# The end of an attention and mixture-of-experts kernel on one core: the turn of the head ahead of the last, the last output copy, and the place of a loop with a run-time count

## The chip, the cores and the metric

The kernel runs on one core of one Trainium2 chip. A core has a matrix engine (TensorE, PE in the rows), a vector engine (VectorE, DVE), an activation engine (ScalarE, ACT), a general engine (GpSimd, POOL) and an engine that mostly issues transfers (SyncE, SP). All of them run their own instruction streams and meet through semaphores. The metric is the device time of one execution in microseconds; the time before is the median of three runs.

## The reference, cut to what matters

```python
# x: (8, 512, 256); attention with 4 groups of 4 query heads, D = 128; experts: 64, the best 6 of each token, room 64
x = x + _layernorm(_L0_attn_ref(_layernorm(x), wq, bq, wkv, bkv, wo))
x = x + _layernorm(_L0_ffn_ref(_layernorm(x), gate_w, w_gate, w_up, w_down, sh_gate, sh_up, sh_down))

# attention: q = x @ wq + bq + pe ; k, v from x @ wkv + bkv (k + pe)
scores = jnp.einsum('bgqtd,bgksd->bgqts', q, k) / math.sqrt(D)          # causal mask follows
probs = jax.nn.softmax(scores, axis=-1)
out = jnp.einsum('bgqts,bgksd->btgqd', probs, v).reshape(b, t, G * QPG * D) @ wo

# feed-forward: softmax over x @ gate_w.T, best 6 experts of each token; each expert takes its first 64 tokens
g = jax.nn.silu(jnp.einsum('ech,ehf->ecf', buf, w_gate)); u = jnp.einsum('ech,ehf->ecf', buf, w_up)
d = jnp.einsum('ecf,efh->ech', g * u, w_down)                            # weighted and added back to the tokens
y = y + (jax.nn.silu(h @ sh_gate.T) * (h @ sh_up.T)) @ sh_down.T         # the shared expert
```

## The kernel before

There are 8 sequences ("batches" below) of 512 tokens and 16 heads, so 128 pairs of batch and head, which the main loop numbers k = 0 to 127. One pass of that loop computes the scores of head k in four row tiles (`scores`, L328: product, mask and minimum on VectorE, exponential with row sums on ScalarE), turns the weights of head k - 1, weighs head k by the reciprocal row sums (`weigh`, L345; on VectorE for the last head alone), projects head k - 3 into the sums of its batch (`project`, L402), computes the queries of head k + 1 and multiplies the turned weights of head k - 2 with the values (`mix`, L390).

Turning means that the weights, tokens in rows, have to stand with keys in rows. For most heads `turned` does it with block transposes on VectorE and a pass through DRAM: four stores `ex_d<-eb` and one load `et<-ex_d` on SP. For the last two heads, 126 and 127, `turned_at_once` transposes on TensorE (L380): ten 128x128 transposes in four groups of 4, 3, 2 and 1, each group into one PSUM buffer of the pool `ps_s`, which has three. ScalarE copies groups 0 and 2 out, VectorE groups 1 and 3. The fourth group therefore waits for the buffer of the first. In the pass of head 127 this call for head 126 stands behind the scores and ahead of `project(124)`. After the loop come `mix(126)`, the projections of 125 and 126, the turn of 127, its product with the values, the copy of that product to SBUF (`ao`, on ScalarE, 128x512) and its projection.

`last_part` then does the feed-forward of the last batch, number 7, mixed with what is left of batch 6. All instructions there stand in a hand-written order (`manual_schedule`), and each engine runs its own in that order. For batch 7: normalization, the shared expert in three chunks of the hidden size (`shared`, L749 and L762; its product with the down matrix in three parts, L728), the routing, and the one pair of experts with free places ("late"): `gather` and `gate_up`, `hid_late`, `turn_hidden` (`pth_late`, `ht_late`), `down` (`pd_late`, then `dd_late` copied by ScalarE), and the last products that add it to the sums `py` (L952). `output6` is a generator that finishes batch 6 in three steps: statistics (VectorE) and the power -0.5 (GpSimd); shift, four scaled rows (ScalarE, L98) and four additions (GpSimd, L694); and the store (SP, L696). In the kernel before, all three steps are called behind `down("late")`, and the generator's last chunk of the shared expert (`next(f)`, the VectorE operations `gs` and `hid` of chunk 0) ahead of them.

At the very end, if more than one pair of experts has free places, a loop with a run-time count (`tc.For_i(0, table["rest"], 1)`, L1073) goes over these other pairs. Each pass recomputes the outputs of batches 5, 6 and 7, so the kernel keeps for it in DRAM the residuals (`x1_d`), the rows with scores and places (`lxg_d`) and the sums (`ly_d`) of those batches. With the inputs given, the count is zero: no line of its body is in the trace. What remains of it is the way around it, on every engine. In the program, SP waits at the way around for the eight semaphores of the transfers that SP and ScalarE issue, then each engine walks a list of twelve waits (all transfers, all engines and their sequencers), and branches on. Behind it stands only the program's end: SP waits for what is open, each engine drains, and two rounds of a barrier follow (L1148).

Of the kernel before, what the change touches and what calls it, by code (L numbers as in the profile page):

```python
# [16 lines left out]
ALU = mybir.AluOpType  # L17
AX = mybir.AxisListType

P = 128  # L20
B, T, E = 8, 512, 256
NT = B * T
NI = T // P
BS = 32
AT = [0, 4, 7, 9]
# [14 lines left out]
EARLY = 5  # L40
# [4 lines left out]
def sandwich_kernel(ctx, tc, x, wq, bq_t, wkv, bk_t, bv, wo, gate_wt, w_gate, w_up, w_down,  # L45
# [63 lines left out]
    def on_act(dst, src):  # L109
        nc.scalar.copy(dst, src)  # L110
# [35 lines left out]
    with ExitStack() as part:  # L146
# [226 lines left out]
        def turned_at_once(k):  # L373

            l = live[k]
            l["et"] = p2.tile([P, NI, NB, BS], F32, tag="et", name=f"et_{k}")
            for j in range(NI):
                pt = ps_s.tile([P, NI, NI, BS], F32, tag="s", name=f"pe_{k}_{j}")
                for i in range(j, NI):
                    nc.tensor.transpose(pt[:, i - j, :, :].rearrange("p a t -> p (a t)"), l["e"][i][:, ts(j, P)], ident)  # L380
                (on_act, on_dve)[j % 2](l["et"][:, :, AT[j] : AT[j] + NI - j, :].rearrange("p a n t -> p n a t"),
                                        pt[:, : NI - j, :, :])

        def mix(k):
            b, h = divmod(k, NH)
            l, g = live[k], h // QPG

            pav = ps_m.tile([P, NI, NI, BS], F32, tag="m", name=f"pav_{k}")
            for j in range(NI):
                nc.tensor.matmul(pav[:, :, j:, :], lhsT=seqs[b]["v"][:, j, ts(g, D)],  # L390
                                 rhs=l["et"][:, :, AT[j] : AT[j] + NI - j, :], start=j == 0, stop=j == NI - 1)
            l["ao"] = p2.tile([D, T], F32, tag="ao", name=f"ao_{k}")
            on_act(l["ao"].rearrange("d (i a t) -> d i a t", i=NI, a=NI), pav.rearrange("d a i t -> d i a t"))
# [492 lines left out]
        def last_part(before, spare):  # L886
# [34 lines left out]
            nc.sync.dma_start(out=rows_of(x1_d, b * T), in_=xt)  # L921
# [18 lines left out]
            next(f)  # L940
# [3 lines left out]
            gate_up_hidden("late")  # L944
            turn_hidden("late")
            l["part"](py, 0)
            down("late")
            output6()
            output6()
            output6()  # L950
            for i in range(NI):
                nc.tensor.matmul(py[i // 2][:, i % 2, :], lhsT=gt[:, ts(i, P)], rhs=pairs["late"]["dd"],  # L952
                                 start=False, stop=True, skip_group_check=True)
            mv, rs = norm_scales([py[i // 2][:, i % 2, :] for i in range(NI)], f"y{b}")
            y = p2.tile([P, NI, E], F32, tag="xnt", name=f"y_{b}")
            for n in range(2):
                nc.scalar.copy(y[:, ts(n, 2), :], py[n])
            nc.sync.dma_start(out=rows_of(ly_d, b * T - ET_ROWS), in_=y)
            for i in range(NI):
                nc.vector.tensor_scalar(o[:, i, :], py[i // 2][:, i % 2, :], mv[:, i, 0:1], None, ALU.subtract)  # L960
            for i in range(NI):
                nc.vector.scalar_tensor_tensor(xt[:, i, :], o[:, i, :], rs[:, i : i + 1], xt[:, i, :],
                                               ALU.mult, ALU.add)
                if i % 2:
                    nc.sync.dma_start(out=rows_of(out, b * T)[:, i - 1 : i + 1, :], in_=xt[:, i - 1 : i + 1, :])
# [32 lines left out]
        for k in range(NK):  # L998
# [10 lines left out]
            if k == NK - 1:  # L1009
                turned_at_once(k - 1)  # L1010
            weigh(k)
            side(s, "A")
            if k >= 3:
                project(k - 3)
# [53 lines left out]
        last_part(behind, routed)  # L1068
# [4 lines left out]
        with tc.For_i(0, table["rest"], 1) as n:  # L1073
# [5 lines left out]
            for b in range(EARLY, B):  # L1079
# [3 lines left out]
                q, tag = [(p1, "y"), (p2, "x"), (p2, "x")][b - EARLY]  # L1083
# [8 lines left out]
            for b in range(EARLY, B):  # L1092
# [7 lines left out]
                for _ in output(b, y, residual(b, p1, "xn")):  # L1100
                    pass

# [49 lines left out]
```

## Time and profile before

| what | value |
|---|---|
| median of three runs | 1431.27 us (1430.13 to 1436.82) |
| profiled execution, its own time | 1429.28 us |
| its span, first to last instruction | 1427.6 us |
| granted TensorE clock, mean over the span | 0.994 |
| TensorE busy | 1383.4 us, 97% of the span |
| VectorE, ScalarE, GpSimd busy | 63%, 35%, 30% |
| last matmul starts / last store issued / last store landed | 1411.8 / 1416.8 / 1420.9 us |

Rows of the timeline give the start, the duration or length of a merged group, the engine, the line, the operation, output and inputs by the program's names with shapes, and in brackets how long the engine stood idle before and what released it. In the table of stretches the numbers after the stretch are its length and then the busy time of PE, PE's weight loads, VectorE, ScalarE and GpSimd, each with its count of instructions; after them the granted clock, the share of DMA time and GB/s. Rows of one line's instructions give a count, the shortest, median and longest duration in ns, and the first and last start. Times of landing are those of the trace's records of transfers, on the same clock.

### The profile page before, as it was taken

What the parts mean: (1) busy time and instruction counts of PE and PEld (TensorE: products, weight loads), DVE (VectorE), ACT (ScalarE), POOL (GpSimd) and SP (SyncE); (2) the same over time, 40 slices, a digit from 0 to 9 for tenths busy, and PEclk for the clock granted to TensorE, in tenths of its full rate; (3) what the DMA queues carried; (4) which work ended last, traced back from release to release, by engine and by line L of the source; (5) the groups of instructions that cost most, each with busy time, mean ns of one, the idle gap of its engine ahead of it and who ended that gap; (6) DMA issues with size and microseconds to landing.
All of it is one profiled execution on the core that took longest, in us unless ns stands there. A gap on an engine that the chain in (4) does not pass through costs nothing.

```text
span 1427.6 us, 18526 instructions
## 1 busy us (share of the span) xinstructions
PE 1383.4 (97%) x5230; PEld 841.4 (59%) x5230; DVE 895.4 (63%) x3127; ACT 500.2 (35%) x1432; POOL 433.7 (30%) x698
## 2 busy tenths in 40 slices
PE   9999999999999999999999999999989999999895
PEld 5665665666556665656556665655546565556463
DVE  5565577656775577557765677566656545677634
ACT  2332344224332334234422433233433333444421
POOL 2222242213321242114221232124545344444311
PEclk9999999999999999999999999999999999999998
DMA  7774566546763576455654566459999889877702
GB/s 243 204 225 146 140 181 198 146 119 171 215 177 107 150 208 193 110 140 164 207 164 125 155 173 193 107 147 276 302 246 258 225 239 252 210 236 250 240 30 82
DMA packets 167990, 262.50 MB, mean 184 GB/s; under 512 B 17212, under 2 KB 142109, under 8 KB 167885
## 3 DMA queue, kind: packets, MB, share of 16 engines
q1 hardware_dynamic: 133069, 212.00, 50.5%
q10 hardware_dynamic: 28672, 39.85, 9.4%
q0 software_dynamic: 6144, 9.44, 3.4%
q8 instruction: 42, 0.69, 0.2%
q14 instruction: 63, 0.52, 0.1%
HBM read 148.25 MB, written 112.99 MB: 183 GB/s over the span
## 4 chain that ended last, share of the span: by engine, by line
PE 80%; DMA 7%; DVE 7%; issue 2%; ACT 2%; POOL 1%; SPq 1%; ACTq 0%; DVEq 0%; POOLq 0%
PE pav L390 16%; PE psc L328 15%; PE pq L315 13%; PE po L402 13%; PE pk L285 4%; PE pv L296 4%; PE psg L749 3%; PE psu L749 3%; PE pgu L590 2%; PE py L776 2%; PE pd L616 2%; DMA wd<-in_w_down 2%; DVE eb L361 1%; DMA exr_d<-xb_f 1%; ACT e L335 1%
## 5 line engine op out<-in xcount | busy, mean ns | idle before, releaser
L345 POOL TENSOR_SCALAR e<-e,recip 128x128 f32<-128x128 f32 x508 | 268.5, 574 | 757.6 <-DVE recip L342 744.0
L335 ACT ACTIVATE e<-e,least 128x128 f32<-128x128 f32 (+3 forms) x512 | 285.8, 559 | 349.2 <-DVE least L332 337.1
L328 PE MATMUL psc<-kt,qt 128*128 128x128 f32 (+3 forms) x1024 | 306.3, 438 | 8.6 <-DVE least L332 6.0
L390 PE MATMUL pav<-et,v 128*128 128x512 f32 (+3 forms) x1024 | 297.5, 434 | 3.3 <-DMA et<-ex_d 3.0
L390 PEld LDWEIGHTS pav<-et,v 128*128 128x128 f32 x1024 | 194.1, 190 | 165.7 <-issue 116.8
L332 DVE CUSTOM_DVE_ANT_0 e<-psc,mask 128x128 f32<-128x128 f32 (+3 forms) x512 | 232.6, 479 | 56.3 <-PE psc L328 49.4
L402 PE MATMUL po<-wo_sb,ao 128*128 128x256 f32 x1024 | 243.5, 381 | 0.7 <-ACT ao L110 0.7
L315 PE MATMUL pq<-xnt,wq_sb 128*128 128x512 f32 x512 | 242.2, 596 | 0.0
L402 PEld LDWEIGHTS po<-wo_sb,ao 128*128 128x128 f32 x1024 | 193.1, 190 | 72.0 <-issue 41.0
L110 ACT COPY ao<-pav 128x512 f32<-128x512 f32 x128 | 74.9, 585 | 443.8 <-PE pav L390 429.6
L361 DVE STREAM_TRANSPOSE eb<-e 128x128 f32<-128x128 f32 x756 | 227.4, 364 | 3.5 <-DMA ex_d<-eb 3.2
L328 PEld LDWEIGHTS psc<-kt,qt 128*128 128x128 f32 x1024 | 164.6, 191 | 76.7 <-DVE least L332 26.9
L318 DVE SCALAR_TENSOR_TENSOR qt<-pq,bq_sb,pe_sb 128x512 f32<-128x512 f32 x128 | 95.6, 747 | 104.6 <-PE pq L315 104.4
L315 PEld LDWEIGHTS pq<-xnt,wq_sb 128*128 128x128 f32 x512 | 96.3, 191 | 69.7 <-issue 64.3
L342 DVE RECIPROCAL recip<-total 128x4 f32<-128x4 f32 x128 | 22.8, 178 | 120.2 <-ACT e L335 120.2
L335 ACT ACTIVATION_READ_ACCUMULATOR e<-e,least 128x1 f32 x512 | 95.8, 187 | 0.0
L627 POOL DMA_INDIRECT y_d<-dd,idx x32 | 50.9, 1591 | 102.0 <-DMA y_d<-dd,idx 51.5
L285 PE MATMUL pk<-xnt,wkv_sb 128*128 128x512 f32 x128 | 59.3, 594 | 0.2 <-ACT xnt L110 0.2
L296 PE MATMUL pv<-wkv_sb,xnt 128*128 128x512 f32 x128 | 58.1, 593 | 0.0
L298 DVE TENSOR_TENSOR v<-pv,bv_sb 128x512 f32<-128x512 f32 x32 | 22.1, 691 | 49.7 <-PE pv L296 49.7
L288 DVE SCALAR_TENSOR_TENSOR kt<-pk,bk_sb,pe_sb 128x512 f32<-128x512 f32 x32 | 24.0, 750 | 44.1 <-PE pk L285 44.1
L113 DVE COPY ht<-pth 88x256 f32<-88x256 f32 x32 | 13.4, 418 | 56.6 <-PE pth L607 56.6
(200 smaller groups left out, 1100.0 us busy)
## 6 DMA issues: line engine op xcount, KB each, us to landing
ex_d<-eb SPq DMA_DIRECT2D x504, 160.0 KB
et<-ex_d SPq DMA_DIRECT2D x126, 640.0 KB
wgu<-in_w_gate ACTq DMA_DIRECT2D x32, 352.0 KB
wgu<-in_w_up ACTq DMA_DIRECT2D x32, 352.0 KB
wd<-in_w_down ACTq DMA_DIRECT2D x32, 352.0 KB
y<-y_d ACTq DMA_DIRECT2D x10, 512.0 KB
x<-in_x SPq DMA_DIRECT2D x8, 512.0 KB
x_d<-x SPq DMA_DIRECT2D x8, 512.0 KB
```

Of the source, the lines that this page charges most:

```text
L285: nc.tensor.matmul(pk, lhsT=wkv_sb[:, c, g, 0, :], rhs=s["xnt"][:, c, :], start=c == 0, stop=c == NC - 1)
L296: nc.tensor.matmul(pv, lhsT=s["xnt"][:, c, ts(i, P)], rhs=wkv_sb[:, c, :, 1, :], start=c == 0, stop=c == NC - 1)
L315: nc.tensor.matmul(pq, lhsT=wq_sb[h // QPG][:, c, ts(h % QPG, D)], rhs=seqs[b]["xnt"][:, c, :], start=c == 0, stop=c == NC - 1)
L318: nc.vector.scalar_tensor_tensor(qt, pq, bq_sb[:, h : h + 1], pe_sb, ALU.add, ALU.add)
L328: nc.tensor.matmul(psc[:, :w], lhsT=l["qt"][:, ts(i, P)], rhs=seqs[b]["kt"][h // QPG][:, :w], start=True, stop=True)
L332: nc.vector.tensor_tensor_reduce(out=e, in0=psc[:, :w], in1=mask[:, T - w :], scale=-1.0 / math.sqrt(D), scalar=BIG, op0=ALU.add, op1=ALU. ...
L335: nc.scalar.activation(e, e, AF.Exp, bias=l["least"][:, i : i + 1], scale=-1.0, accum_out=l["total"][:, i : i + 1])
L345: engine.tensor_scalar(e, e, recip[:, n : n + 1], 1.0, ALU.mult, ALU.mult)
L361: nc.vector.transpose(blocks.rearrange("p c j t -> p j c t"), l["e"][i][:, js[0] * P : (js[-1] + 1) * P].rearrange("p (j c t) -> p j c t", ...
L390: nc.tensor.matmul(pav[:, :, j:, :], lhsT=seqs[b]["v"][:, j, ts(g, D)], rhs=l["et"][:, :, AT[j] : AT[j] + NI - j, :], start=j == 0, stop=j ...
L402: nc.tensor.matmul(po[b][i // 2][:, i % 2, :], lhsT=ao[:, ts(i, P)], rhs=wo_sb[:, h, :], start=h == 0 and i % 2 == 0, stop=h == NH - 1, sk ...
L749: nc.tensor.matmul(as_taken(pp[:mw, :], xt2), lhsT=w_sb[:, c, ds(f0, mw)], rhs=in_order(xt2, c), start=c == 0, stop=c == NC - 1)
```

## The change

Four things are edited.

1. In the pass of head 127, `project(124)` goes ahead of the turn of head 126, and all four copies of that turn are made by VectorE.
2. The copy of the last head's product (`ao` of head 127) is made in two halves, the first by VectorE, the second by ScalarE.
3. In `last_part`, the three steps of `output6` are spread: the first behind `gate_up("late")`, the second behind the last chunk of the shared expert, which itself moves behind `gate_up_hidden("late")`, the third ahead of `down("late")`.
4. The last products, the normalization and the output of batch 7 become a function of their own, `last_output`, which is called behind the loop over other pairs. The loop adds its products for batch 7 to the sums in PSUM instead of recomputing that batch from DRAM. So the stores of batch 7 to `x1_d` and `ly_d` and the copies ahead of the latter fall away, and one tile in the loop takes another pool.

```diff
-        def turned_at_once(k):
+        def turned_at_once(k, evictions=(on_act, on_dve) * 2):
...
-                (on_act, on_dve)[j % 2](l["et"][:, :, AT[j] : AT[j] + NI - j, :].rearrange("p a n t -> p n a t"),
-                                        pt[:, : NI - j, :, :])
+                evictions[j](l["et"][:, :, AT[j] : AT[j] + NI - j, :].rearrange("p a n t -> p n a t"),
+                             pt[:, : NI - j, :, :])
...
-            on_act(l["ao"].rearrange("d (i a t) -> d i a t", i=NI, a=NI), pav.rearrange("d a i t -> d i a t"))
+            ao, rows = l["ao"].rearrange("d (i a t) -> d i a t", i=NI, a=NI), pav.rearrange("d a i t -> d i a t")
+            if k < NK - 1:
+                on_act(ao, rows)
+            else:
+                on_dve(ao[:, :2], rows[:, :2])
+                on_act(ao[:, 2:], rows[:, 2:])
...
-            nc.sync.dma_start(out=rows_of(x1_d, b * T), in_=xt)
...
             gate_up("late")
-            next(f)
+            output6()
             py = l["py"] = [ps_o.tile([P, 2, E], F32, tag=f"o{n}", name=f"py_{b}_{n}") for n in range(2)]
             l["part"](py, 2)
             l["part"](py, 1)
             gate_up_hidden("late")
+            next(f)
+            output6()
             turn_hidden("late")
             l["part"](py, 0)
+            output6()
             down("late")
-            output6()
-            output6()
-            output6()
-            for i in range(NI):
-                nc.tensor.matmul(py[i // 2][:, i % 2, :], lhsT=gt[:, ts(i, P)], rhs=pairs["late"]["dd"],
-                                 start=False, stop=True, skip_group_check=True)
+            return py, xt, gt, pairs["late"]["dd"]
+
+        def last_output(py, x1, gt, dd):
+            b = B - 1
+            for i in range(NI):
+                nc.tensor.matmul(py[i // 2][:, i % 2, :], lhsT=gt[:, ts(i, P)], rhs=dd, start=False, stop=True,
+                                 skip_group_check=True)
             mv, rs = norm_scales([py[i // 2][:, i % 2, :] for i in range(NI)], f"y{b}")
             y = p2.tile([P, NI, E], F32, tag="xnt", name=f"y_{b}")
-            for n in range(2):
-                nc.scalar.copy(y[:, ts(n, 2), :], py[n])
-            nc.sync.dma_start(out=rows_of(ly_d, b * T - ET_ROWS), in_=y)
-            for i in range(NI):
-                nc.vector.tensor_scalar(o[:, i, :], py[i // 2][:, i % 2, :], mv[:, i, 0:1], None, ALU.subtract)
...
+            for i in range(NI):
+                nc.vector.tensor_scalar(y[:, i, :], py[i // 2][:, i % 2, :], mv[:, i, 0:1], None, ALU.subtract)
+            for i in range(NI):
+                nc.vector.scalar_tensor_tensor(x1[:, i, :], y[:, i, :], rs[:, i : i + 1], x1[:, i, :], ALU.mult, ALU.add)
                 if i % 2:
-                    nc.sync.dma_start(out=rows_of(out, b * T)[:, i - 1 : i + 1, :], in_=xt[:, i - 1 : i + 1, :])
+                    nc.sync.dma_start(out=rows_of(out, b * T)[:, i - 1 : i + 1, :], in_=x1[:, i - 1 : i + 1, :])
...
             if k == NK - 1:
-                turned_at_once(k - 1)
+                project(k - 3)
+                turned_at_once(k - 1, (on_dve,) * NI)
             weigh(k)
             side(s, "A")
-            if k >= 3:
+            if 3 <= k < NK - 1:
                 project(k - 3)
...
-        last_part(behind, routed)
+        sums, *last = last_part(behind, routed)
         order.close()
...
-                q, tag = [(p1, "y"), (p2, "x"), (p2, "x")][b - EARLY]
+                q, tag = [(p1, "y"), (p2, "x"), (p1, "xt2")][b - EARLY]
...
-            for b in range(EARLY, B):
+            for i in range(NI):
+                nc.tensor.matmul(sums[i // 2][:, i % 2, :], lhsT=gts[-1][:, ts(i, P)], rhs=pairs["late"]["dd"],
+                                 start=False, stop=False, skip_group_check=True)
+            for b in range(EARLY, B - 1):
...
+        with tc.manual_schedule(engines={ET.PE, ET.DVE, ET.Activation, ET.Pool, ET.SP}):
+            last_output(sums, *last)
```

More of the change, by code (lines that the diff above doesn't have):

```diff
@@ L944, in last_part @@
             gate_up_hidden("late")
+            next(f)
+            output6()
             turn_hidden("late")
             l["part"](py, 0)
+            output6()
             down("late")
-            output6()
-            output6()
-            output6()
+            return py, xt, gt, pairs["late"]["dd"]
+        def last_output(py, x1, gt, dd):
+            b = B - 1
             for i in range(NI):
-                nc.tensor.matmul(py[i // 2][:, i % 2, :], lhsT=gt[:, ts(i, P)], rhs=pairs["late"]["dd"],
-                                 start=False, stop=True, skip_group_check=True)
+                nc.tensor.matmul(py[i // 2][:, i % 2, :], lhsT=gt[:, ts(i, P)], rhs=dd, start=False, stop=True,
+                                 skip_group_check=True)
             mv, rs = norm_scales([py[i // 2][:, i % 2, :] for i in range(NI)], f"y{b}")
             y = p2.tile([P, NI, E], F32, tag="xnt", name=f"y_{b}")
-            for n in range(2):
-                nc.scalar.copy(y[:, ts(n, 2), :], py[n])
-            nc.sync.dma_start(out=rows_of(ly_d, b * T - ET_ROWS), in_=y)
             for i in range(NI):
-                nc.vector.tensor_scalar(o[:, i, :], py[i // 2][:, i % 2, :], mv[:, i, 0:1], None, ALU.subtract)
+                nc.vector.tensor_scalar(y[:, i, :], py[i // 2][:, i % 2, :], mv[:, i, 0:1], None, ALU.subtract)
             for i in range(NI):
-                nc.vector.scalar_tensor_tensor(xt[:, i, :], o[:, i, :], rs[:, i : i + 1], xt[:, i, :],
-                                               ALU.mult, ALU.add)
+                nc.vector.scalar_tensor_tensor(x1[:, i, :], y[:, i, :], rs[:, i : i + 1], x1[:, i, :], ALU.mult, ALU.add)
                 if i % 2:
-                    nc.sync.dma_start(out=rows_of(out, b * T)[:, i - 1 : i + 1, :], in_=xt[:, i - 1 : i + 1, :])
+                    nc.sync.dma_start(out=rows_of(out, b * T)[:, i - 1 : i + 1, :], in_=x1[:, i - 1 : i + 1, :])
         EARLY_TAGS = [(p3, "wgu"), (p3, "wd")]
```

## The prediction

> **What bounds the kernel now.** Read the page's busy shares and slices first, then the stretches at the end of the span, since every edit but one acts after 1352 us.
>
> ```profile
> PE 1383.4 (97%) x5230; PEld 841.4 (59%) x5230; DVE 895.4 (63%) x3127; ACT 500.2 (35%) x1432; POOL 433.7 (30%) x698
> ...
> PE   9999999999999999999999999999989999999895
> ```
>
> TensorE bounds the span: 97% busy, and only the last slices sag. The table of stretches says where:
>
> ```profile
> 1352.00:1358.30 6.30, 4.08 (x20) 2.90 (x21) 3.38 (x13) 4.67 (x14) 2.79 (x4) 1.00 0.58 192
> 1358.30:1372.60 14.30, 13.44 (x60) 9.94 (x60) 1.82 (x5) 2.67 (x5) 0.00 (x0) 1.00 0.00 1
> 1372.60:1403.00 30.40, 30.17 (x127) 17.63 (x125) 19.12 (x62) 8.66 (x21) 3.95 (x6) 1.00 0.18 61
> ...
> 1410.20:1417.70 7.50, 1.99 (x8) 1.43 (x8) 5.37 (x18) 3.02 (x6) 3.93 (x6) 0.89 0.36 122
> 1417.70:1427.60 9.90, 0.00 (x0) 0.00 (x0) 0.00 (x0) 0.00 (x0) 0.00 (x0) 0.50 0.21 71
> ```
>
> PE (second number) is full from 1358 to 1410. It loses 2.2 us in the first stretch, and in the last 17.4 us it has 2 us of work. In the final 9.9 us no engine computes. The timeline of the first stretch:
>
> ```profile
> 1352.64 0.34 SPq L371 DMA_DIRECT2D et<-ex_d  x1
> ...
> 1352.87 1.39 PE L380 MATMUL pe<-ident,e 128*128 128x128 f32 x9
> ...
> 1355.84 0.83 ACT L110 COPY et<-pe 128x512 f32<-128x512 f32 x2
> ...
> 1356.46 0.33 PE L380 MATMUL pe<-ident,e 128*128 128x128 f32 x1 [2.19 <-ACT et L110]
> ...
> 1356.62 1.89 PE L402 MATMUL po<-wo_sb,ao 128*128 128x256 f32 x8
> ...
> 1358.35 4.48 PE L390 MATMUL pav<-et,v 128*128 128x512 f32 x16
> ```
>
> The tenth transpose needs the PSUM buffer of the first four. ScalarE empties it only at 1355.84, behind four exponentials. The end, from the timeline and the rows of the closing line L1148 and of the loop's line L1073:
>
> ```profile
> 1407.36 1.39 DVE L78 BATCH_NORM_STATS2 st_y<-y 128x6 f32<-128x256 f32 x4
> ...
> 1410.19 1.99 PE L952 MATMUL py<-dd_late,gt 128*128 128x256 f32 x8 [0.47 <-ACT dd_late L110]
> ...
> 1414.07 1.02 POOL L88 TENSOR_TENSOR rs_y<-ve_y,mhalf 128x4 f32<-128x4 f32 x1
> 1414.14 0.38 SPq L696 DMA_DIRECT2D out_dram<-x  x1
> 1414.57 0.51 SPq L958 DMA_DIRECT2D ly_d<-y  x1
> ...
> 1416.04 1.63 SPq L965 DMA_DIRECT2D out_dram<-x  x2
> ```
>
> ```profile
> L1148 POOLq DRAIN  x3: 46/103/5303, 1421.4 to 1427.3; - x3
> ...
> L1073 PEldq EVENT_SEMAPHORE  x13: 51/51/51, 1412.2 to 1421.2; - x13
> ```
>
> The loop makes no pass (none of its body's lines is in the trace), yet all engines stand in its waits until the last store has landed: 1420.94 by the landing records. Only then does GpSimd reach its drain of 5.30 us, and 0.84 us of closing events follow. From the first last product P to the end are 1427.57 - 1410.19 = 17.38 us.
>
> **The change, part by part.** Places are on the clock of the old trace.
>
> *The turn of head 126.* The projection of head 124 (8 matmuls, 1.73 us by their starts; its ao has been ready since 1350.6) goes ahead of the transposes. It begins at 1353.03 after the last score and ends at 1354.75. Nine transposes 0.11 us apart follow. VectorE's first copy, 512 wide (0.69 us, by its copy o_xt<-pt_f of that shape), can start at about 1355.35 and frees the buffer at 1356.05, so the tenth ends by 1356.3. Next are the products of head 125, whose et was issued at 1352.64 and landed at 1356.72. So a wait for a DMA takes the stall's place: they start at 1356.85, not 1358.35. Gain 1.50; 2.0 if the load is earlier, 1.2 if it lands 0.3 later. VectorE gains two copies, 0.69 and about 0.42 (its 256-wide copy gxt_late), and weighs head 127 by 1358.8, where the transposes that read it start near 1364.6. That cover of 5.8 us makes them free; without it they cost 1.1.
>
> *The last output copy in two.* Before, ScalarE's 0.58 us copy starts at 1369.97 and PE resumes at 1370.61. After, VectorE copies half (0.42) and the first four matmuls go. ScalarE's half is ordered behind VectorE's by a wait in the program, 0.05 + 0.37 (its 256-wide copy dd_late); PE wants it 0.86 us after the first half. It is hidden, so the gain is 0.16 (bounds 0 and 0.25). Together 1.66, and PE's and VectorE's chain to 1409.7 moves by that, its content unchanged.
>
> *Batch 6's output.* Its four statistics move from 1407.36 to behind gxt_late, at 1401.56: with aggregation and sum (0.36 + 0.17) over at 1403.43. hid_late (2 x 0.34) follows at 1403.5, then gs and hid of chunk 0 (2 x 0.68) until 1405.6. PE needs that chunk at 1406.8 and a buffer it frees at 1406.6: 1.0 us of cover, past which PE waits one for one. GpSimd's power (1.02) runs meanwhile. shift_y then stands at 1405.6 instead of 1410.42; from it to the store were 3.72 us (ScalarE 4 rows, GpSimd 4 adds), so the store is issued at 1409.3, less 1.66: 1407.7. ScalarE's rows are over before it needs pd_late at 1409.72. On SP the x1 store (0.36 us of issue, landed long before) goes and frees nothing that is late.
>
> *The loop ahead of the last products.* A new wall: nothing after it starts until that store has landed. 512 KB stores in this quiet stage landed 2.89, 3.01 and 3.03 us after issue (1382.89, 1392.51, 1414.14): T = 1410.7. PE, whose dd_late is ready at 1408.5, is queued behind the wall. In the old trace PE needed 0.71 us from the last landing to its first instruction behind the loop; the store now sits on an earlier semaphore with four more events of 0.106 us to walk. So P = T + 1.15 = 1411.8: 1.6 us later than before.
>
> Two rules of the Trainium skill speak against this place. *Runtime: NRT & Kernel Launch, Instruction fetch mechanics* says that a taken branch to a page outside the engine's two-page window stalls until it is fetched. The trace has the same exits: 0.16 to 0.57 us from branch to next event, code fetches of 8 KB lasting 0.3 to 0.55 us. By the row the walk above holds it; by the rule add a fetch, for which the nearest row is 1.94 us (a 128 KB store from issue to landing), mostly covered because PE arrives 3 us early. I take 0, with 2 kept as the end. *TensorE: Matmul & The Clock Gate, Part 1*, says that an idle window of about 3.4 us halves the clock. The trace shows it:
>
> ```profile
> 965.35 3.08 PE pq L315 x4
> ```
>
> Four such matmuls take 1.72 us elsewhere; the granted clock was 0.5 there, and it fell again 3.9 us after PE's last work at the end. By the rule's windows, PE's new gap (1408.06 to 1411.8, 3.7 us) holds a whole one about 1 time in 10. Then the products cost about 1.5 us more; I take 0, with 1.5 kept.
>
> *The tail behind P.* The chain to the last issue was 1416.83 - P = 6.64. The power waited 0.42 us for GpSimd's adds, which are now done earlier, so VectorE's four subtractions set the pace: 6.46. The ly store and its two ScalarE copies (1.04 us, not on this chain) go. Before, 1.5 MB of stores queued at about 340 GB/s, and the last landed 4.1 us after issue; 512 KB alone should land in about 2.3 (between 1.94 for 128 KB and 2.9 for 512 KB). That gives P + 8.8, and P + 9.8 with the closing 0.84 and SP's events. But GpSimd's last work ends at P + 4.45, its drain begins at about P + 4.75 with no wait before it, and 5.30 us later it has become the later one: P + 10.05, with closing P + 10.9. So the tail shrinks by 6.5. Here *VectorE: DVE Perf Modes, The DRAIN you can't avoid*, puts closing drains at about 12 ns on all engines; the row has 5303 ns on GpSimd, and the row decides. By the page the end would be P + 9.8.
>
> **Sum.** P at +1.6, tail -6.5: -4.8 to -4.9; I take -4.8. The profiled execution had a span of 1427.6 and a time of 1429.28; it becomes 1422.8 and 1424.5. The median of the runs shown, 1431.27, stood 2.0 above the profiled one, and is carried: 1426.5. The measurement can tell about 0.5%, 7.2 us, from no change, so this is "same".
>
> **Rivals.**
> - *The drain stays exposed.* If the 5.30 us begin only when all stores are in, the end is P + 8.8 + 0.45 + 5.3 + 0.84, P + 15.4: -0.4, 1430.9. For it: it began 0.5 us after the last landing. Against: nothing in the program makes GpSimd wait there. Chance 0.14.
> - *The drain is short* when GpSimd comes from work rather than from the loop: P + 9.8, -5.9, 1425.4. Chance 0.14.
> - *The turn gains nothing*, the et load landing late (it took 4.1 us from issue; the one for head 122, under more traffic, 4.3), or chunk 0 outlives its 1.0 us: -3.3, 1428.0. Chance 0.12.
> - *Slower: the way out of the loop is the cost.* If the 5.30 us at L1148 are not a drain but GpSimd's price for coming out of the loop to code it does not hold, and PE pays the like, P moves by 5.3 and the sum is +0.5: 1431.8, more with the clock halved. It decides from a stall of 4.8 us on. Against: PE, DVE and ACT left in under 0.3 us. Chance 0.06.
> - The likeliest, as summed: 0.54.
>
> **Numbers.** Range 1423.2 to 1431.2: below, a short drain with the full 2.0 of the turn and some scatter of the medians (1430.13 to 1436.82 were shown); above, the exposed drain. Outside are the slower case and half of the others' edges. Faster by over 0.5% (under 1424.1) needs 2.4 us beyond the sum: 0.14. Slower by over 0.5% (over 1438.4): 0.06. Between: 0.80.
>
> **What would show it.** The transposes' wait on ACT et L110 is gone, and the products of head 125 start near 1356.9 after a wait for et<-ex_d. Every row from 1372 to 1406 stands 1.5 to 1.7 us earlier. The out_dram store of batch 6 is issued near 1407.7, the last products start near 1411.8 at a clock of 1.0, GpSimd's long drain starts before the last stores are issued or just after, and the span ends 11 us behind the products. I am wrong if the store leaves after 1412, if PE idles over 2 us between landing and products, or if the drain begins after the last landing.

## The result, and the profile after

The changed kernel takes 1426.43 us (median of 20 runs, 1421.94 to 1431.36), the kernel before 1431.28 beside it (20 runs, 1425.37 to 1436.82): ratio 0.9972, interval 0.996 to 0.9984. Measured again later on one chip with the last experiment it took 1426.25 (16 runs) against 1430.00, ratio 0.9979 (0.9968 to 0.999). By the medians it is faster by 4.9 and 3.8 us, by the two ratios by some 4.0 and 3.0, which is under the 0.5% that counts as a difference here. The profiled execution took 1426.9 us with a span of 1425.2, against 1429.28 and 1427.6: 2.4 us less.

The page's busy shares and TensorE's slices (tenths of each fortieth of the span):

```profile
PE 1384.5 (97%) x5230; PEld 841.7 (59%) x5230; DVE 893.7 (63%) x3130; ACT 498.3 (35%) x1428; POOL 433.1 (30%) x698
...
PE   9999999999999999999999999999999999999996
```

TensorE still bounds the span, and only the last slice sags, with 6 in place of 5. What has changed is at the end. The stretches of the changed kernel, cut at its own events (columns: stretch, its length, busy time with instruction counts of PE, PEld, DVE, ACT and POOL, the clock granted to TensorE, the DMA share, GB/s):

```profile
1352.00:1357.20 5.20, 4.21 (x21) 3.05 (x21) 3.31 (x12) 4.06 (x12) 2.79 (x4) 1.00 0.57 191
...
1408.90:1412.85 3.95, 0.00 (x0) 0.00 (x0) 0.00 (x0) 0.36 (x1) 0.00 (x0) 0.89 0.41 141
1412.85:1419.10 6.25, 3.78 (x8) 2.50 (x8) 3.16 (x13) 0.00 (x0) 1.02 (x1) 0.50 0.00 1
1419.10:1425.20 6.10, 0.00 (x0) 0.00 (x0) 1.96 (x5) 0.00 (x0) 0.00 (x0) 0.50 0.25 86
```

Three things are new. A stretch of 3.95 us has opened ahead of the last products in which no engine but ScalarE does anything, for 0.36 us: everybody stands at the loop. The eight products behind it take 3.78 us where before had 1.99, at a clock of 0.50. And the last stretch is 6.1 us long and still has 1.96 us of VectorE in it; VectorE's last addition ends at 1421.06, so that the time in which no engine computes is 4.1 us, where it was 9.9.

The turn, from the timeline:

```profile
1352.30 0.34 SPq L371 DMA_DIRECT2D et<-ex_d  x1
...
1352.99 1.89 PE L407 MATMUL po<-wo_sb,ao 128*128 128x256 f32 x8
...
1354.72 1.15 PE L380 MATMUL pe<-ident,e 128*128 128x128 f32 x9
...
1355.35 1.68 DVE L113 COPY et<-pe 128x512 f32<-128x512 f32 x4 [1.46 <-PE pe L380]
...
1356.10 0.33 PE L380 MATMUL pe<-ident,e 128*128 128x128 f32 x1 [0.24 <-DVE et L113]
...
1357.15 1.12 PE L390 MATMUL pav<-et,v 128*128 128x512 f32 x2 [0.72 <-DMA et<-ex_d]
```

The tenth transpose waits 0.24 us for VectorE in place of 2.19 for ScalarE. What is late next is the load of et, 0.72 us: it landed at 1357.11 by the landing records, 4.8 us after its issue (4.1 in before). Counted from the start of the last score matmul, to take out what the execution lost or won earlier, the products of head 125 begin at 4.59 us and not at 5.91.

The last output copy in two halves, and the end:

```profile
1369.25 0.42 DVE L113 COPY ao<-pav 128x256 f32<-128x256 f32 x1 [2.29 <-PE pav L390]
1369.70 0.37 ACT L110 COPY ao<-pav 128x256 f32<-128x256 f32 x1 [3.12 <-DVE ao L113]
...
1369.73 1.56 PE L407 MATMUL po<-wo_sb,ao 128*128 128x256 f32 x6 [0.94 <-DVE ao L113]
```

```profile
1408.29 0.38 SPq L701 DMA_DIRECT2D out_dram<-x  x1
1408.89 0.37 ACT L110 COPY dd_late<-pd_late 128x256 f32<-128x256 f32 x1 [2.01 <-PE pd_late L621]
...
1412.85 3.78 PE L960 MATMUL py<-dd_late,gt 128*128 128x256 f32 x8 [4.01 <-SPq L1079]
...
1417.99 1.02 POOL L88 TENSOR_TENSOR rs_y<-ve_y,mhalf 128x4 f32<-128x4 f32 x1 [9.73 <-DVE ve_y L86]
...
1420.29 1.17 SPq L969 DMA_DIRECT2D out_dram<-x  x2
```

dd_late is copied at 1409.26, yet the first last product waits for SP's event at the loop, L1079, until 1412.85: batch 6's store landed at 1411.74 and PE had 1.11 us more to go. The rows of the loop and of the closing line (operation, count, shortest, median and longest in ns, first and last start):

```profile
L1079 PEldq EVENT_SEMAPHORE  x13: 51/51/51, 1408.9 to 1412.4; - x13
```

```profile
L1159 POOLq DRAIN  x3: 46/109/6383, 1418.0 to 1424.9; - x3
```

The first row now lies ahead of the products, where it lay behind them. The second is GpSimd's drain. It is entered at 1417.96, just ahead of the power, so its 6383 ns hold that power too; it ends at 1424.34, 5.33 us after the power's end. The last two stores had landed at 1422.46 and 1423.24. So the drain is still the last thing, but it lies over the subtractions, the stores and their landing, where before it followed them.

### The profile page after: what moved, and what is told of

It reads as the page before. It is cut to its first block, busy times and chain, and to the rows that moved or that the text cites. A ratio compares the mean times of both kernels' runs of the same rounds, so it can differ in the third digit from the quotient of the medians.

```text
span 1425.2 us, 18521 instructions
## 1 busy us (share of the span) xinstructions
PE 1384.5 (97%) x5230; PEld 841.7 (59%) x5230; DVE 893.7 (63%) x3130; ACT 498.3 (35%) x1428; POOL 433.1 (30%) x698
## 5 line engine op out<-in xcount | busy, mean ns | idle before, releaser
L361 DVE STREAM_TRANSPOSE eb<-e 128x128 f32<-128x128 f32 x756 | 227.4, 364 | 1.8 <-DMA ex_d<-eb 1.5
```

The lines of the kernel that those rows point to most:

```text
L361: nc.vector.transpose(blocks.rearrange("p c j t -> p j c t"), l["e"][i][:, js[0] * P : (js[-1] + 1) * P].rearrange("p (j c t) -> p j c t", ...
```

## The experiments

Executions scatter by several us before any of this: the last score matmul starts anywhere from 1348.8 to 1360.3 us in the profiles of kernels whose work up to there is the same. So each profile is cut into three intervals, read off the starts of the same matmuls: from the last score to the last projection (head 127), from there to the first last product, and from that to the end (which holds the eight products, whose length stands in a column of its own).

| kernel | score to projection | projection to product | eight products take | product to end | ratio of times to before |
|---|---|---|---|---|---|
| before | 18.17 | 39.58 | 1.99 | 17.37 | 1 |
| changed | 17.17 | 43.12 | 3.78 | 12.34 | 0.9972 (0.996 to 0.9984) |
| e1_turn | 15.97 | 39.58 | 1.99 | 17.36 | 0.9988 (0.9973 to 1.0003) |
| e2_loop | 19.87 | 42.93 | 3.56 | 12.12 | 0.9985 (0.9972 to 0.9998) |
| e3_one_copy | 16.80 | 42.98 | 2.93 | 11.49 | (one run) |
| e4_out_last | 16.17 | 47.99 | 3.42 | 11.98 | 1.0018 (1.0004 to 1.0032) |
| e5_power_act | 17.18 | 43.03 | 3.49 | 11.29 | 0.9993 (0.9982 to 1.0003) |
| e6_busy | 17.42 | 46.57 | 3.61 | 12.17 | 0.9999 (0.9982 to 1.0017) |
| e7_store_behind | 16.43 | 41.27 | 3.38 | 11.95 | 0.9965 (0.9953 to 0.9978) |
| e8_ly | 17.55 | 42.95 | 3.78 | 12.34 | 0.9985 (0.997 to 1.0) |
| e9_busy2 | 17.23 | 43.17 | 1.99 | 10.56 | 0.9969 (0.9952 to 0.9985) |
| e10_halves | 16.87 | 42.49 | 3.78 | 12.34 | 0.9947 (0.993 to 0.9963) |
| e11_best | 17.14 | 42.75 | 2.47 | 10.28 | 0.9954 (0.9936 to 0.9972) |
| e12_after_again | 17.14 | 43.04 | 3.61 | 12.17 | 0.9979 (0.9968 to 0.999) |

Two sums of this table say most. Counted from the end of the eight products, the tail is 15.4 us in before and e1_turn, 8.56 or 8.57 in every kernel with the new end and GpSimd's power in it, and 7.8 in the two that take the power from GpSimd (e5_power_act, e11_best). And from the last score to the end the changed kernel's trace takes 72.63 us for 75.12: the tail gives 6.8 and the turn with the copy 1.0, the later first product takes 3.5 back and the slower products 1.8.

**The theory and its rivals.** Mine: the gain is the turn's 1 us or so plus GpSimd's drain going under the tail, less what the wall at the loop costs (a later first product, and the clock). Rivals: the turn carries it; the store that was dropped carries it; the drain lies under the tail by accident or is not constant. One rival has no run: that the earlier output of batch 6 would have gained as much with the loop left in its old place (taken up under "Where the wall stands").

### The turn alone, the end alone

```diff
# e1_turn, on the kernel before
...
+                project(k - 3)
-                turned_at_once(k - 1)
+                turned_at_once(k - 1, (on_dve,) * NI)
...
-            if k >= 3:
+            if 3 <= k < NK - 1:
```

> The kernel before with the first edit alone (projection of head 124 ahead of the last turn, four copies on VectorE); the end of the kernel is that of before. Theory A (the tail carries most of the gain): the products of head 125 start about 1.2 us earlier, and everything behind them too, so 1.2 us less in all, ratio 0.9992; GpSimd's drain still begins only after the last store has landed, with 17.4 us from the first last product to the end. Rival B (the restart after the last turn carries the gain): most of the 4.85 us, ratio near 0.997. Rival C (the turn's gain is lost at the next wait): no change, 1.000.

```diff
# e2_loop, on the changed kernel
-                project(k - 3)
-                turned_at_once(k - 1, (on_dve,) * NI)
+                turned_at_once(k - 1)
...
-                on_dve(ao[:, :2], rows[:, :2])
-                on_act(ao[:, 2:], rows[:, 2:])
+            on_act(ao, rows)
```

> The changed kernel with the turn of head 126 and the single copy of the last ao as before; only the end is changed (output of batch 6 earlier, the loop ahead of the last products, no store of the last batch's partial sums). Theory A: 3.5 to 4.5 us less than before, ratio 0.997 to 0.9975; first last product near 1414, end 12.3 us after it in an execution where the products run at half clock, 10.7 where they do not. Rival B (the gain is the turn's): within 1 us of before, ratio above 0.999. In both the store of batch 6 is issued about 0.9 us later than in the changed kernel.

Both ratios miss 1 by about as much, 1.2 and 1.5 in a thousand (1.7 and 2.1 us), and together they make about the changed kernel's 2.8. The turn alone has 1 within its interval, and both intervals are 2.6 to 3.0 in a thousand wide, so that the times alone settle neither the rival "it is all the turn" nor my figure of 3.5 to 4.5 us for the end. The intervals of the traces do: in e2_loop the last two sum to 55.05, against 56.95 of before, 1.9 less, and in e1_turn they are those of before. Both parts gain, and the end gains half of what I had said. I had written down the difference of medians and not added up the trace, in which the changed kernel gains 1.5 there. (The 19.87 of e2_loop holds a half-clock stretch of TensorE, 1359.58 to 1363.0. It follows one, from 1356.17, in which the old turn's wait for ScalarE, 2.20 us here, left TensorE 36% of work. In before that wait fell across two such stretches, with 68% and 48% of work, and the clock was kept. So the old turn could cost the clock as well, by where its wait fell; see "The clock of the last products".)

The timeline of e1_turn shows what the turn is worth when nothing is late behind it:

```profile
1359.00 0.33 PE L380 MATMUL pe<-ident,e 128*128 128x128 f32 x1 [0.24 <-DVE et L113]
1359.17 4.48 PE L390 MATMUL pav<-et,v 128*128 128x512 f32 x16
```

There et was issued 1.51 us ahead of the last score and landed in time; no wait stands before pav, which starts 3.71 us after the last score, 2.2 sooner after it than in before. In every profile with the new turn, pav starts either there (3.70 in e4_out_last) or 0.04 us after et has landed: 3.85 to 4.97 in the others. The load decides, and the gain, counted from the last score, is 0.9 to 2.2.

### One copy of the last output

```diff
# e3_one_copy, on the changed kernel
-            if k < NK - 1:
-                on_act(ao, rows)
-            else:
-                on_dve(ao[:, :2], rows[:, :2])
-                on_act(ao[:, 2:], rows[:, 2:])
+            on_act(ao, rows)
```

> The changed kernel with the last ao copied by ScalarE alone, in one copy, as before. Theory A (VectorE's half starts 0.4 us late because it waits in a separate instruction ahead of it): the last projection starts 0.2 us earlier after the end of its products than in the changed kernel, 0.7 us after the last product's end in place of 0.94. Rival B (the prediction's step: two halves are shorter than one whole): it starts 0.16 us later, 1.1 us after. The time of the whole kernel cannot tell 0.2 us.

```profile
1369.23 0.59 ACT L110 COPY ao<-pav 128x512 f32<-128x512 f32 x1 [2.30 <-PE pav L390]
1369.87 0.92 PE L403 MATMUL po<-wo_sb,ao 128*128 128x256 f32 x3 [0.73 <-ACT ao L110]
```

PE waits 0.73 us for one whole copy and 0.94 for the first of two halves. The copy of half the size is shorter by 0.17, but it starts 0.46 us after the last product's end, and ScalarE's 0.09. On both engines the wait for PE is an instruction of its own; ScalarE's copy starts 0.06 us after it, VectorE's 0.42 us. The separate wait by itself is not the reason, though the expectation took it for one: ScalarE has it too, and VectorE's block transpose at L361 starts 0.05 us after such a wait in the changed kernel's trace. What keeps VectorE here is open. The split costs 0.2 us.

### Where the wall stands

```diff
# e4_out_last, on the changed kernel: batch 6's three steps behind down("late")
             gate_up("late")
-            output6()
...
-            output6()
             turn_hidden("late")
...
             down("late")
+            output6()
+            output6()
+            output6()
```

> The changed kernel with the three steps of batch 6's output put back behind the last down product, so that its store is issued about 5 us later. Theory A (all engines stand in the loop's wait list until that store has landed): the first last product starts about 5 us later, near 1417.5, the products run at half clock after some 8 us of an idle TensorE, and the end is 4 to 5 us later than the changed kernel's, so about the time of before, ratio 0.999 to 1.001. Rival B (the loop's wait is hidden by something else, such as the drain): no more than 1 us later than the changed kernel, ratio 0.997 to 0.998.

```profile
1404.15 0.37 ACT L110 COPY dd_late<-pd_late 128x256 f32<-128x256 f32 x1 [6.30 <-PE pd_late L621]
1408.52 0.38 SPq L701 DMA_DIRECT2D out_dram<-x  x1
...
1412.97 3.42 PE L960 MATMUL py<-dd_late,gt 128*128 128x256 f32 x8 [8.87 <-SPq L1079]
```

The store stands 43.54 us after the last projection, in place of 38.56, and the first product 47.99 in place of 43.12: 4.98 and 4.87, nearly one for one. PE waits 8.87 us with its data ready. The time is that of before, or a little more. So the loop's new place without the earlier output of batch 6 does not pay; the drain does not hide the wall.

The other half is not shown: no run has the earlier output of batch 6 with the loop in its old place. In before the last two stores landed 3.80 and 4.11 us after their issue, in line behind those of batch 6 and of ly_d; in e8_ly below, with ly_d's store alone ahead of them, 2.19 and 2.16. By these numbers, as an estimate, the earlier output alone would bring the last landing, and with it the old loop's end, some 1.9 us forward, which is all that e2_loop gains in its trace. At half clock the loop's new place may thus have gained nothing of its own.

```diff
# e7_store_behind, on the changed kernel
             l["part"](py, 0)
-            output6()
             down("late")
...
-                q, tag = [(p1, "y"), (p2, "x"), (p1, "xt2")][b - EARLY]
+                q, tag = [(p1, "y"), (p1, "xg"), (p1, "xt2")][b - EARLY]
...
         with tc.manual_schedule(engines={ET.PE, ET.DVE, ET.Activation, ET.Pool, ET.SP}):
+            store6()
             last_output(sums, *last)
```

> The changed kernel with the store of batch 6's output issued behind the loop (which holds only for a loop without a pass; marks of the loop's body use another buffer). Theory A (the landing of that store is what the loop's waits last for): the first last product starts about 1.1 us after the end of the copy of dd, 40.6 us after the last projection's start in place of 43.0, TensorE idles under 2 us so that the products run at full clock, and the end comes 2.4 to 4 us earlier than the changed kernel's, ratio to before 0.995 to 0.996. Rival B (the loop's entry itself costs that time: branches, registers, the engines' handshake): the first product stays near 43 us after the last projection's start.

```profile
1409.40 0.37 ACT L110 COPY dd_late<-pd_late 128x256 f32<-128x256 f32 x1 [2.00 <-PE pd_late L621]
1410.07 0.38 SPq L701 DMA_DIRECT2D out_dram<-x  x1
1411.52 3.38 PE L959 MATMUL py<-dd_late,gt 128*128 128x256 f32 x8 [2.16 <-issue]
```

Without a landing to wait for, the first product comes 1.85 us earlier after the last projection, not 2.4: 41.27, not 40.6. PE's wait has become "issue", 2.16 us: its own walk through the loop's waits, which it begins when its last matmul is through. That is the floor of this place. The clock stayed at half, against the expectation. The times, not taken side by side, differ by 1.8 us in the mean (1424.93 and 1426.73) and by 1.4 in the median.

### What the drain counts from

```diff
# e5_power_act, on the changed kernel
-            mv, rs = norm_scales([py[i // 2][:, i % 2, :] for i in range(NI)], f"y{b}")
+            st = small.tile([P, NI, 6], F32, tag="st", name="st_last")
+            for i in range(NI):
+                nc.vector.bn_stats(st[:, i, :], py[i // 2][:, i % 2, :])
...
+            nc.vector.tensor_scalar_add(ve, mv[:, :, 1], EPS)
...
+            nc.scalar.activation(rs, ve, AF.Sqrt)
...
+            nc.vector.reciprocal(rs, rs)
```

> The changed kernel with the last power taken from GpSimd: ScalarE takes the square root of the variance, VectorE the reciprocal; GpSimd has nothing to do behind the loop. Theory A (the drain counts from GpSimd's last work, whatever the others still do): it begins at the loop's exit and ends some 5.3 us later, inside the tail; the end is then set by the landing of the last store and comes 0.8 to 1.2 us earlier counted from the first last product (11.2 in place of 12.3 at half clock, 9.7 in place of 10.6 at full clock). Rival B (the 5.3 us are paid behind the last event of all engines, and lay under the tail by accident): end at least 16 us after the first last product. Rival C (the drain is short once GpSimd has been idle): the same end as theory A, but a drain far under 5 us.

```profile
L1169 POOLq DRAIN  x3: 46/103/5303, 1419.6 to 1430.9; - x3
```

With nothing left for GpSimd behind the loop, its drain begins at the loop's exit, 1419.57, and lasts 5303 ns, the very figure of before, though GpSimd's last work had ended at 1415.38, 4.2 us earlier. So the drain counts from where it is entered, or from the end of a work still under way there (5.33 us after the power's end in the changed kernel). It is over at 1424.88, while the last store lands at 1430.18. The end stands 11.29 us after the first product, in place of 12.34: theory A. Of that microsecond 0.29 is the clock (the products took 3.49 for 3.78), and 0.76 the power's move. Rivals B and C fall, the one by the end, the other by the 5303 ns. The time did not show it: 1427.41 in 14 runs, interval with 1 in it; that the edit shortens the kernel is shown for the tail of the trace alone.

```diff
# e8_ly, on the changed kernel
...
+            for n in range(2):
+                nc.scalar.copy(copy[:, ts(n, 2), :], py[n])
+            nc.sync.dma_start(out=rows_of(ly_d, b * T - ET_ROWS), in_=copy)
```

> The changed kernel with the two copies of ScalarE and the store of the last batch's partial sums put back behind the last products, as before had them. Theory A (they lie beside VectorE's chain and beside the drain): the last two stores land up to 1 us later, and the end comes 0 to 1 us later. Rival B (leaving them out is what brought the gain: a store of 0.5 MB off the queues): 3 to 4.5 us later, the time of before.

```profile
1420.44 0.58 ACT L966 COPY y_copy<-py 128x512 f32<-128x512 f32 x1 [1.12 <-DVE st_y L78]
1421.05 0.38 SPq L967 DMA_DIRECT2D ly_d<-y_copy  x1
1423.27 1.17 SPq L973 DMA_DIRECT2D out_dram<-x  x2
```

In this place the dropped store was no gain. Put back, it leaves at 1421.05 and lands 2.91 us later, 0.7 us after the first of the other two was issued. These land 2.19 and 2.16 us after their issue, as they do without it (2.17 and 2.15). From product to end it is 12.34 in both.

### The clock of the last products

```diff
# e6_busy (6 of them) and e9_busy2 (2), on the changed kernel
             down("late")
+            busy = ps_s.tile([P, T], F32, tag="s", name="busy")
+            for _ in range(6):
+                nc.tensor.matmul(busy, lhsT=ident, rhs=xt[:, :2, :].rearrange("p i e -> p (i e)"), start=True, stop=True)
```

> The changed kernel with six matmuls of 128x512 into a scratch buffer behind the last down product, so that TensorE idles about 1.4 us in place of 4.0 ahead of the last products. Theory A (TensorE's gap in the loop's wait costs the last products their clock): the products take 2.0 us and not 2.9 to 3.8, the end is 10.6 to 10.7 us after the first of them, and the time 1 to 1.7 us less than the changed kernel's, ratio to before 0.996 to 0.997. Rival B (the half clock falls there anyway, a matter of the execution): the products at 2.9 to 3.8 us again, and no change. In both the first product starts where it did.

```profile
1416.80 5.42 PE L957 MATMUL busy<-x,ident 128*128 128x512 f32 x12
1424.32 3.61 PE L963 MATMUL py<-dd_late,gt 128*128 128x256 f32 x8 [2.10 <-issue]
```

A miss by its own size: each of the six is two passes of 0.43 us in the trace, so they lasted 5.42 us, PE reached the loop's waits late, and 2.1 us of its own walk followed. The first product came 3.45 us later, still at half clock.

> The changed kernel with two scratch matmuls of 128x512 (each is two of 0.43 us in the trace) behind the last down product, so that TensorE idles 2.3 us ahead of the last products in place of 4.0, and does not reach the loop's waits too late (six, of 5.2 us together, did that). Theory A (TensorE's clock halves in a stretch of 3.41 us that follows one in which it was busy for about a third or less; 59% was enough in before): where the stretches of this execution leave it over half busy, the eight products take 2.0 us and the end is 10.6 us after the first; otherwise 2.9 to 3.8 and 11.5 to 12.3 as before. The first product is at most 0.3 us later than the changed kernel's 43.1 us after the last projection's start. Time 0 to 1.7 us less. Rival B (the clock at that place has nothing to do with what TensorE did): half clock in the products as in all kernels with the loop ahead of them.

```profile
1406.57 1.98 PE L957 MATMUL busy<-x,ident 128*128 128x512 f32 x4
1410.69 1.99 PE L963 MATMUL py<-dd_late,gt 128*128 128x256 f32 x8 [2.14 <-SPq L1082]
```

With two, the products start where they did (43.17) and take 1.99 us, and the end is 10.56 us behind them: the 1.8 us are the clock.

The half clock comes in stretches of 3.41 us: within each trace, the changes of the granted clock lie a multiple of that apart. Laid on this grid, all fourteen traces, from end to end, agree. After a stretch at full clock in which TensorE was busy for 43% or less, the next was at half clock, in 42 cases of 42; after one with 56% and more in none of 5670. Between 45% and 55% both came (half in 8 of 36). From half clock it came back after a stretch with 85% of work and more (36 of 36), and not after 82% and less (none of 33). Ahead of the last products the changed kernel has 7%, e6_busy 38%, e7_store_behind 37%, e11_best 41%, and e9_busy2 47%. The last four have gaps of much the same length, 2.1 to 2.2 us, so that e9_busy2 kept its clock in part by where its stretches lay: the gap fell across two of them, with 47% and 58%. (The 59% that its expectation gives for before are 71% on this grid.)

### Half stores, and all together

```diff
# e10_halves, on the changed kernel
...
+            halves = [(0, NI)] if b < B - 2 else [(0, 2), (2, NI)]
+            for first, end in halves:
+                for i in range(first, end):
                     nc.gpsimd.tensor_add(x1[:, i, :], x1[:, i, :], y[:, i, :])
+                if end < NI:
+                    nc.sync.dma_start(out=rows_of(out, b * T)[:, :end, :], in_=x1[:, :end, :])
...
```

> The changed kernel with the output of batch 6 stored in two halves of 0.25 MB, the first behind the second of GpSimd's four additions. Theory A (the landing of the last byte of batch 6 lets the loop go, and half the size lands in about 2.2 us as the two last stores did, not 3.4): the second half lands about 1.2 us sooner, the first last product starts 41.9 us after the last projection's start in place of 43.1, the end comes 1.2 us earlier; ratio to before 0.996 to 0.9975. Rival B (a store's latency is fixed, not a matter of its size): no change. Rival C (TensorE's own walk through the wait list, 1.9 us behind its last matmul, takes over): the gain stops at the point where the first product stands 1.9 us behind the down products' end, about 41.2 us after the last projection's start.

```profile
1405.42 0.38 SPq L703 DMA_DIRECT2D out_dram<-x  x1
1406.25 1.08 PE L621 MATMUL pd_late<-wd_late,ht_late 88*64 88x256 f32 x8
1406.78 0.38 SPq L705 DMA_DIRECT2D out_dram<-x  x1
1410.70 3.78 PE L964 MATMUL py<-dd_late,gt 128*128 128x256 f32 x8 [3.37 <-SPq L1083]
```

Theory A by its sign, with half its size: the second half landed 2.91 us after its issue (the first 2.97 after its own), not 2.2. The first product is 0.63 us earlier. That two halves overlap is not the reason: the last two stores overlap too, and landed in 2.19 and 2.18 us. One difference stands in the queues of this stretch (queue, kind: packets, MB, share of the DMA engines):

```profile
q1 hardware_dynamic: 544, 0.52, 30.2%
q14 instruction: 3, 0.02, 1.8%
q8 instruction: 1, 0.02, 1.5%
```

Fetches of code, 8 and 16 KB each, run beside these stores, and around the last two there are none. The changed kernel's store of batch 6 has such fetches beside it too, and it took 3.45 us, where a store of its size took 3.01 at 1391.63 with none beside it. That the fetches hold the last packets back fits, but no run tests it. The time of e10_halves was the lowest of all, 1423.21, but in only 6 runs.

```diff
# e11_best: e3_one_copy, e5_power_act and e10_halves, and
+            for _ in range(3):
+                nc.tensor.matmul(busy[:, :E], lhsT=ident, rhs=xt[:, 0, :], start=True, stop=True)
```

> What the runs so far point to, together: the changed kernel with the last ao in one copy, the power of the last batch on ScalarE and VectorE, batch 6's output stored in two halves, and three scratch matmuls of 128x256 (0.43 us each) behind the last down product. Theory A, by its parts as measured: last projection 0.2 us earlier after its products, the first last product 42.3 us after the last projection's start (43.1 in the changed kernel, 42.5 with the halves alone), products 2.0 us, GpSimd's drain over before the last store has landed, and the end 9.6 us after the first product (10.6 with GpSimd's power, 12.3 at half clock). In all 3 to 4 us less than the changed kernel, ratio to before 0.994 to 0.996. Rival B (the parts share one gain, so that they do not add): within 1.5 us of the changed kernel.

> The changed kernel as it is, beside the combination on the same chip: ratio to before 0.997 to 0.9985, half clock in the last products (2.9 to 3.8 us), the first last product 43.0 to 43.2 us after the last projection's start, the end 11.5 to 12.4 us after it. What the combination is worth is read against this run.

```profile
1408.05 1.56 PE L957 MATMUL busy<-x,ident 128*128 128x256 f32 x6
...
1411.75 2.47 PE L963 MATMUL py<-dd_late,gt 128*128 128x256 f32 x8 [2.14 <-issue]
```

```profile
L1172 POOLq DRAIN  x3: 46/103/5303, 1411.2 to 1421.8; - x3
```

The combination took 1425.21 us (8 runs) beside 1426.25 for the changed kernel again and 1430.00 for before: ratios 0.9954 and 0.9979, whose intervals overlap, so that it beats before but not surely the changed kernel. In the traces, from the last projection to the end, it takes 53.03 us against 55.21, 2.2 less. Of the 3 to 4 us that were expected, 2.2 came in the traces and 1.0 in the medians. Two things fell short: the scratch matmuls now were the later ones (the wait is 2.14 of "issue", and the landing at 1410.43 was over), so the first product came at 42.75 and not 42.3, and the clock fell in the middle of the products, after a stretch with 41% of work.

## Why the prediction was right or wrong

The predicted median, 1426.5, is the measured one, 1426.4; the sum behind it was not that good. On the profiled execution it forecast 1422.8 of span and 1425.2 came. Of these 2.4 us the clock took 1.8, the smaller shift from the turn and the copy 0.7, and the landing of batch 6's store 0.3; the tail apart from the clock gave 0.3 back. They were made up by the 2.0 us that was carried from the profiled execution to the median. That 2.0 came from three runs. In the comparison with the changed kernel the median of before kept it (1431.28, 20 runs); beside the experiments, with 16 to 51 runs each, it was 1429.2 to 1430.0, hardly above its profiled 1429.28. And the changed kernel's median lies 0.5 below its profiled execution, not 2.0 above. So the direction and the parts were foreseen, but the agreement to 0.1 us is luck.

- *The turn* was right by mechanism: the wait on ScalarE went, and the load of et took its place. 1.50 was forecast, 1.32 came (1.2 to 2.0 was the range), because the load took 4.8 us and not 4.1; it was issued 0.27 us ahead of the last score, where before it was 0.20 behind it, or more would have been lost.
- *The copy in two* was wrong in sign: 0.16 forecast, -0.2 measured against the single copy. The step that failed is that VectorE starts like ScalarE after PE; it started 0.37 us later. The forecast shift of 1.66 for the chain became 1.0 from score to projection: 1.3 of the turn less 0.2 of the split, with 0.1 unaccounted for.
- *Batch 6's output* held: the store was to leave 38.75 us after the last projection and left after 38.56. The cover of chunk 0 was enough.
- *The wall* held, as e4_out_last and e7_store_behind show. T to P was 1.11 us for 1.15: the fetch stall that was weighed did not show on PE's way out of the loop. The store's landing was mis-sized, 3.45 us for 3.0; with all terms P came 0.27 us later against the projection than forecast.
- *The clock* is the step that failed most. The prediction took the rule of the Trainium skill (*TensorE: Matmul & The Clock Gate, Part 1*: after an idle window of about 3.4 us the clock halves) to need a window idle from end to end, and gave a gap of 3.7 us one chance in ten. The products were at half clock, whole or in part, in all nine profiles that have the loop ahead of them and no scratch work, after windows with up to half of work in them. The gap was 4.0 us; however the windows fall, one of them gets 2 us of it or more, that is, 41% of work or less where the rest is full, and no window with so little kept the clock. The price was 1.8 us in the changed kernel's profile. Page and trace agree on the length of the windows (3.41 us) but not on "idle". The trace of before could have told: the half clock that the prediction shows, at 965.35, follows a stretch in which TensorE was busy for a third.

```profile
962.15:965.56 3.41, 1.14 (x6) 0.59 (x5) 0.84 (x4) 1.40 (x4) 1.69 (x4) 1.00 1.02 338
965.56:968.98 3.42, 3.42 (x5) 1.33 (x4) 0.89 (x3) 0.00 (x0) 2.33 (x3) 0.50 1.02 366
```

- *The drain* was right, in size and in what it lies over. The figure it was weighed against (*VectorE: DVE Perf Modes, The DRAIN you can't avoid*: about 12 ns) is given there for the drains that the runtime adds ahead of a kernel and behind it; the drains here stand on the program's own closing line, and GpSimd's took 5.30 us from its entry, or 5.33 from the end of its power. Without the clock the end would have been 10.56 us behind P (e9_busy2), for 10.9 forecast.

So the rival "the drain stays exposed" fell by the changed kernel's own trace and by e5_power_act, "the drain is short" by the same two, and "the turn gains nothing" by e1_turn's and the changed kernel's traces. The slower rival, a stall on leaving the loop, did not come.

What is left open: what decides the clock between 45% and 55% of work, why VectorE needed 0.42 us behind its wait, what delays a store's landing ahead of the loop, and what the loop's new place is worth over the earlier output of batch 6 alone.

## What to carry to other kernels

A wait of all engines can cost the engine that bounds the kernel twice: first the later of the last landing and its own walk through the waits, then its clock behind the gap. Before one is moved, look what still lands there, and issue that first and in smaller pieces. And look which engine has the longest closing work, and let it begin that early: it is then hidden under the others' work, as most of GpSimd's 5.3 us were.

## What the hardware showed that was not expected

- TensorE's clock halved after every stretch of 3.41 us with up to 43% of work in it (42 of 42 in fourteen traces), not only after idle ones, and after none with 56% and more.
- GpSimd's closing drain lasts 5.30 us from its entry, or ends 5.33 us after a power still under way there, and runs beside other engines' work and stores.
- VectorE's copy of half of ao started 0.42 us after its wait, 0.46 after the product; ScalarE's whole copy in the same place 0.06 and 0.09.
- PE's walk through a loop without a pass takes 2.10 to 2.16 us from its last matmul to its next, where no landing is later (e6_busy, e7_store_behind, e11_best).
- 0.25 MB stores landed 2.85 to 3.22 us after issue ahead of the loop (e10_halves, e11_best) and 2.15 to 2.19 at the new end of the kernel, two under way at once in both places; 0.5 MB took 3.31 to 3.45 ahead of the loop and 2.91 behind it (e8_ly), and 4.30 where code was fetched beside it (e7_store_behind).
